# An LSTM's input products in groups of 32 steps with 26 outer products, instead of 24 steps with 20

## The chip, the cores and the metric

The kernel runs on one core of one Trainium2 chip. The metric is the device time of one execution in microseconds. In the texts and in the profile PE is TensorE (PEld its weight loads), DVE is VectorE, ACT is ScalarE, POOL is GpSimd and SP is SyncE, which issues all transfers here.

## What is computed

A residual around an LSTM layer in fp32: 32 sequences, 512 steps, 512 inputs, 512 hidden units, so 2048 gate columns. Cut to what matters:

```python
xW = einsum('ntd,dg->ntg', x, Wx) + b          # (32, 512, 2048)
def step((h, c), xw_t):
    a = xw_t + h @ Wh                          # the recurrent product
    i, f, o = sigmoid(a[:, :H]), sigmoid(a[:, H:2*H]), sigmoid(a[:, 2*H:3*H])
    g = tanh(a[:, 3*H:])
    c = f * c + i * g
    h = o * tanh(c)
    return (h, c), h
out = x + scan(step, (cond_1024, 0), xW)       # all h, added to x
```

`h @ Wh` can only be done step by step. `x @ Wx` has no such chain, and the kernel computes it for whole groups of steps ahead of their use, by a scheme that needs fewer multiplications than the plain product.

## The kernel before

**One step.** `h_part(t)` (L269) multiplies the last h by `wh_sb` into a PSUM bank that already holds that step's `x @ Wx + b` (16 matmuls of 512 columns, which the trace shows as 32). `cell(t)` follows (L284 to L295): two sigmoids and a tanh on ACT, the products and sums on DVE (`prod` L288, L289, L293), and the transposes (L295) that make the next step's h. While the cell runs, TensorE works on the stream of products for later steps (`emit_matmuls`, L548). TensorE's order in a step is the h part of the step, then a portion of the stream.

**The stream.** Steps 20 to 499 go in groups (`GS` steps, `NG` groups). A group's x is cut into blocks, and an outer bilinear algorithm of `R` slots gives its products: each slot multiplies one combination U of x blocks (`U_OF`, `U_SUMS`) by one combination V of weight blocks (`V_OF`, `V_SUMS`), and the output blocks are combinations W of the slots' results (`W_OF`, `W_SUMS`). Inside a slot a second algorithm with 7 products is used (`ROW`), so a slot is 7 products and a group `7 * R`. The position in the stream, `pos`, counts quarter products, 28 a slot. Each step issues as many as the group needs on average, rounded to even numbers: 22 or 24 a step.

**What DVE and ACT do for it.** `pair_sum` (L509 to L515) makes the four sums inside the x blocks. `u_op` (L453) makes a U. `evacuate` takes results out of the banks into buffers: three copies on ACT (L594, L603, L610) and three additions on DVE (L600, L604, L607) a slot. `w_op` (L418) makes the W. Finished output blocks are stored to DRAM (`store_blocks`, L434); `load_xw` (L663) brings them back three steps ahead of their use, and `seed_step` (L674) copies them into the step's bank on ACT. The bias comes in by copies on ACT (`seed_banks`, L578) that put a combination of bias rows in the bank of certain slots (`BIAS_OF`).

**Orders.** The order of work on each engine is the order of the program (`manual_schedule`). A budget decides how many W are made in a step: `room["dve"]` starts at 3800, each operation takes `150 + 1.05 * columns` off, and W are issued while more than 1000 is left; what does not fit waits in `wqueue`. In a step the evacuations come first, then U, pair sums and W, then the portion of the stream, then the cell. SP issues every transfer in the order of the program, and a transfer also waits for the one eight places earlier.

**V.** The V combinations are made once, at the start (`v_add`, L711), and stored to DRAM (`v_store`, L715): 768 + 128 KB for a sum, 384 + 128 KB for a slot whose V is a plain weight block (`V_DIRECT`). `load_v` (L639, L644) loads row after row into a ring of three.

**The head.** Steps 0 to 19 have `x @ Wx` computed plainly (`plain_block`, L202), since no group is ready. `HEAD_PLAINS` says which plain step is computed in which step. `keep` adds the bias on DVE to its bank: in place (L804), or into a buffer that waits in SBUF (L807), or into one that goes out to the DRAM tensor `kept` (L811, L812). The stream starts in step 6 with the portions of `HEAD_STREAM`; from `STREAM0` on a step has the steady portion. While the head runs, `load_group` (L500) loads the first x blocks, with the stores of V ahead of it on SP's queue.

**The tail.** The stream ends at step 472 (`END`); from 474 (`SPLIT`) on each step is done in two halves, so that the cell of one half runs beside the matmuls of the other. The last 12 steps are plain again (`plain_part`, L211), computed in portions as filler in the split steps, with weights that `late_loads` (L223) bring back in the steps listed in `LATE`. Their bias is added on DVE when the last portion of a step is done.

Of the kernel before, what the change touches and what calls it, by code (L numbers as in the profile page):

```python
# [24 lines left out]
GS = 24  # L25
NG = 20
TAIL = T - HEAD - NG * GS
R = 20
TAU = (1, 0, 2)
# [4 lines left out]
AHEAD = 28  # L34
# [3 lines left out]
LATE = (454, 456, 458, 460, 462, 470, 471)  # L38
# [6 lines left out]
V_FIRST = (1,)  # L45
V_NEXT = (3,)
V_STEPS = ((4, 5, 7), (8, 10), (11, 12, 13, 14), (15, 16, 17))
V_ROOMS = (0, 1, 2, 3, 4, 5, 2, 1, 3, 0, 4, 5, 3, 2)

U_SUMS = {6: {3: 1, 5: -1}, 7: {1: 1, 6: 1}, 8: {2: 1, 3: -1}, 9: {2: 1, 7: -1}, 10: {0: 1, 1: -1}, 11: {0: 1, 4: -1}}  # L50
U_OF = [
# [4 lines left out]
]  # L56
V_SUMS = {8: {0: 1, 4: 1}, 9: {3: 1, 7: 1}, 10: {5: 1, 8: -1}, 11: {6: 1, 8: -1}, 12: {6: 1, 9: 1}, 13: {5: 1, 9: -1}}
V_OF = [
# [4 lines left out]
]  # L63
W_SUMS = {
    20: {6: -1, 13: 1}, 21: {1: 1, 7: -1}, 22: {12: -1, 9: 1}, 23: {1: 1, 4: -1}, 24: {16: 1, 20: 1},
    25: {3: 1, 23: 1}, 26: {14: 1, 22: 1}, 27: {15: 1, 24: 1}, 28: {9: 1, 21: 1},
}
W_OF = [
# [3 lines left out]
]  # L72
BIAS_OF = {1: "b3", 3: "b1-b3", 8: "b2+b3", 11: "b2-b0", 13: "b0", 17: "b1-b0"}
# [29 lines left out]
def kernel(  # L103
# [22 lines left out]
    NC = 11  # L126
# [5 lines left out]
    ubuf = const.tile([P, 6, 7, P], F32, name="ubuf")  # L132
    xs0 = const.tile([P, 6, 8, P], F32, name="xs0")
    xs1 = r1[:, 0:6].rearrange("p a b c -> p (a b c)").rearrange("p (k s m) -> p k s m", k=6, s=8)
    xs = [xs0, xs1]
    xnat = const.tile([P, 3, TC, NJ, B], F32, name="xnat")
    seeds_own = const.tile([P, 2, W], F32, name="seeds_own")
    seeds = [r1[:, 6 + i // 2, i % 2 * 2 : i % 2 * 2 + 2].rearrange("p s c -> p (s c)") for i in range(4)]
    seeds += [seeds_own[:, i] for i in range(2)]
# [4 lines left out]
    xwd = [dram.tile([6, P, NJ, W], F32, name=f"xwd_{i}") for i in range(2)]  # L144
# [3 lines left out]

    EXTRA = {NC + 1: 3, NC + 2: 5, NC + 3: 1}
    extra_from = {NC + 1: (7, 0), NC + 2: (10, 5), NC + 3: (13, 0)}  # L150
    lent = []
    retired = []

    def buf_of(i):
        if i in EXTRA:
            return xs0[:, EXTRA[i]].rearrange("p s m -> p (s m)").rearrange("p (s c) -> p s c", s=4)
        return spare if i == NC else cbuf[:, i]

    def lend():
        for i, (made, row) in extra_from.items():  # L160
            if i not in lent and u_made[0] >= made and pos[0] >= 28 * row:
                lent.append(i)
                free_c.append(i)

    def retire():
        for i in lent:
            if i in free_c:
                free_c.remove(i)
                retired.append(i)
# [18 lines left out]
    late_r = xs0.rearrange("p k s m -> p k (s m)").rearrange("p k (s c) -> p k s c", s=4)  # L188

    def raw(blk):  # L190

        return (late_r if late_weights[0] and blk < 6 else r1)[:, blk]

    def plain_block(t, c, bank):

        ko, ki = divmod(c, 2)
        for j in range(NJ):
            w = raw(ko * 4 + j)
            dst = bank[j * B : (j + 1) * B]
            pieces = [(dst[:, 0:HW], w[:, 2 * ki + 1]), (dst[:, HW:W], w[:, 2 * ki])]  # L200
            for n, (d, m) in enumerate(pieces):
                nc.tensor.matmul(  # L202
                    d, x_of(t)[:, c], m, start=c == 0 and n == 0, stop=True, skip_group_check=True
                )
# [15 lines left out]
    def late_load(c, a, b):  # L220
        rows = wx[c].rearrange("p (j s c) -> p j s c", j=NJ, s=2)
        dst = late_r if a < 6 else r1
        return lambda: nc.sync.dma_start(  # L223
            out=dst[:, a:b, c % 2 * 2 : c % 2 * 2 + 2], in_=rows[:, a % 4 : a % 4 + b - a]
        )

    late_loads = [late_load(0, 0, 4), late_load(1, 0, 4), late_load(2, 4, 6), late_load(3, 4, 6)]
    late_loads += [lambda: nc.sync.dma_start(out=seeds_own[:, 0], in_=x[NCHUNK - 2][:, TC // 2 * P : TC * P])]
    late_loads += [late_load(2, 6, 8), late_load(3, 6, 8)]
# [89 lines left out]
    free_c = [*range(6), 8, 9, 10]  # L319
    last_x = []  # L320
    free_u = [2, 3, 4, 5, 0, 1]
# [11 lines left out]
    class Group:  # L333

        def __init__(self, g):
# [12 lines left out]
            for terms in [*U_SUMS.values(), *U_OF]:  # L348
                for i in terms:
                    if i > 5:  # L350
                        self.u_uses[i] = self.u_uses.get(i, 0) + 1
            self.u_slot = {}
            self.stored = [0, 0, 0]
# [91 lines left out]
    def u_block(gr, i):  # L445
        if i < 6:
            return flat(xs[gr.g % 2][:, i, 1:8])
# [290 lines left out]
    def v_slot(s):  # L738

        terms = V_OF[s]  # L740
        for i in terms:
            v_sum(i)
# [339 lines left out]
```

## Time and profile before

| | |
|---|---|
| time, median of 3 runs | 3108.54 us (3107.48 to 3110.77) |
| the profiled execution | 3108.65 us, of which span 3106.9 us |
| busy: PE, DVE, ACT, POOL | 3090.9, 2231.1, 1453.0, 232.3 us |
| moved by DMA | 760.40 MB, mean 245 GB/s |
| granted TensorE clock | full, in every slice of the span |
| starts of steps 0, 6, 20, 474 | 29.9, 88.5, 226.5, 2930.2 us |

The time of a run is 1 to 2 us longer than the span that the profile shows. A row of the list of groups gives line, engine and operation, out<-in with sizes, the count, then busy time and mean ns of one, then the idle time of the engine just before and what ended it. A row of the timeline gives start and length in us, and in brackets the idle time before. A row of the chain gives start, length and what the time went to. Busy TensorE is modelled from the ends of matmuls, so the starts of weight loads (PEld) are the better clock for its pace.

### The profile page before, as it was taken

The numbers are of one execution on the slowest core, as the hardware profiler recorded it, in microseconds if no ns is written. First come the engines' busy times: TensorE is split into PE (matmuls) and PEld (weight loads), VectorE is DVE, ScalarE is ACT, GpSimd is POOL, SyncE is SP. The second block draws the span as 40 slices with busy tenths as digits, with TensorE's granted clock in tenths as the row PEclk, the third lists the DMA queues.
The fourth block names the chain that finished last, engine by engine and source line by source line (L and its number), as shares of the span: only waits on it lengthen the run. The fifth ranks groups of instructions, "written<-read, shape, count | busy, mean of one in ns | idle before, by whom it ended". The sixth has DMA issues, their size and how long they took to land.

```text
span 3106.9 us, 109307 instructions
## 1 busy us (share of the span) xinstructions
PE 3090.9 (99%) x44064; PEld 1662.3 (54%) x44064; DVE 2231.1 (72%) x6217; ACT 1453.0 (47%) x5486; POOL 232.3 (7%) x508
## 2 busy tenths in 40 slices
PE   9999999999999999999999999999999999999999
PEld 6555555555555555555555555555555555555565
DVE  7587776767676777767676767677776767677644
ACT  1344444444444444444444444444444444444444
POOL 0000000000000000000000000000000000000010
PEclk9999999999999999999999999999999999999999
DMA  8788878787877778777877778787877777778630
GB/s 315 253 289 284 276 234 260 236 263 239 261 252 251 255 244 269 243 256 234 267 240 261 251 250 254 242 265 246 265 236 257 242 256 251 255 253 275 197 91 21
DMA packets 315274, 760.40 MB, mean 245 GB/s; under 512 B 50064, under 2 KB 98192, under 8 KB 314256
## 3 DMA queue, kind: packets, MB, share of 16 engines
q1 hardware_dynamic: 314768, 753.40, 74.6%
q8 instruction: 348, 5.70, 0.8%
q14 instruction: 158, 1.29, 0.1%
HBM read 576.26 MB, written 179.31 MB: 243 GB/s over the span
## 4 chain that ended last, share of the span: by engine, by line
PE 97%; DVE 1%; DMA 1%; ACT 0%; issue 0%; SPq 0%; DVEq 0%; ACTq 0%
PE gbank L269 54%; PE xbank L548 33%; PE bbank L548 5%; PE xbank L269 2%; PE xbank L211 1%; PE xbank L202 1%; PE gbank L202 1%; DMA vdram<-vring 0%; PE xbank L839 0%; DMA vring<-vdram 0%; PE bbank L202 0%; DVE prod L288 0%; DVE s L289 0%; DVE hbuf L293 0%; DVE ubuf L453 0%
## 5 line engine op out<-in xcount | busy, mean ns | idle before, releaser
L269 PE MATMUL gbank<-wh_sb,ht 128*32 128x512 f32 (+1 forms) x16256 | 1781.8, 576 | 1.9 <-DVE ht L295 1.1
L269 PEld LDWEIGHTS gbank<-wh_sb,ht 128*32 128x32 f32 x16256 | 609.6, 110 | 828.0 <-issue 704.1
L548 PE MATMUL xbank<-vring,ubuf 128*32 128x256 f32 (+1 forms) x15464 | 956.6, 364 | 4.7 <-ACT cbuf L610 4.0
L284 ACT ACTIVATE s<-gbank 128x128 f32<-128x128 f32 x978 | 274.7, 281 | 1278.7 <-PE gbank L269 1278.2
L548 PEld LDWEIGHTS xbank<-vring,ubuf 128*32 128x32 f32 x15464 | 591.7, 110 | 363.3 <-issue 188.6
L288 DVE TENSOR_TENSOR prod<-s 128x128 f32<-128x128 f32 x1024 | 293.9, 287 | 619.0 <-ACT s L285 618.9
L418 DVE TENSOR_TENSOR cbuf<-cbuf 128x1024 f32<-128x1024 f32 x401 | 482.5, 1216 | 1.4
L303 POOL TENSOR_TENSOR oc<-xnat,ht 128x128 f32<-128x128 f32 x504 | 232.1, 461 | 2835.6 <-DVE ht L295 1471.7
L291 ACT ACTIVATE tanh_c<-s 128x64 f32<-128x64 f32 x1024 | 262.3, 256 | 245.9 <-DVE s L289 241.8
L295 DVE STREAM_TRANSPOSE ht<-hbuf 128x64 f32<-128x64 f32 x1022 | 250.8, 245 | 74.7 <-DVE hbuf L293 1.4
L674 ACT COPY gbank<-xw 128x512 f32<-128x512 f32 x464 | 279.3, 602 | 0.2
L289 DVE TENSOR_TENSOR s<-prod 128x64 f32<-128x64 f32 x1024 | 230.4, 225 | 35.2
L293 DVE TENSOR_TENSOR hbuf<-o,tanh_c 128x64 f32<-128x64 f32 x1024 | 213.1, 208 | 28.8 <-ACT tanh_c L291 28.4
L594 ACT COPY cbuf<-xbank 128x512 f32<-128x512 f32 x370 | 216.0, 584 | 33.2 <-PE xbank L548 18.3
L285 ACT ACTIVATE s<-gbank 128x64 f32<-128x64 f32 x978 | 226.6, 232 | 0.0
L604 DVE TENSOR_TENSOR cbuf<-xbank,cbuf 128x256 f32<-128x256 f32 x370 | 151.6, 410 | 77.9 <-ACT cbuf L603 76.1
L548 PE MATMUL bbank<-vring,ubuf 128*32 128x256 f32 (+1 forms) x2704 | 200.6, 355 | 0.0
L548 PE MATMUL xbank<-vring,xs 128*32 128x256 f32 (+1 forms) x2472 | 173.8, 373 | 2.6 <-ACT xbank L578 1.9
L548 PE MATMUL xbank<-vring,r 128*32 128x256 f32 (+1 forms) x2480 | 173.8, 372 | 0.0
L286 ACT ACTIVATE o<-gbank 128x128 f32<-128x128 f32 (+1 forms) x508 | 155.5, 306 | 0.0
L607 DVE TENSOR_TENSOR cbuf<-xbank,cbuf 128x256 f32<-128x256 f32 x370 | 150.4, 407 | 0.0
L600 DVE TENSOR_TENSOR cbuf<-bbank,cbuf 128x256 f32<-128x256 f32 x370 | 150.0, 405 | 0.1
(114 smaller groups left out, 1804.4 us busy)
## 6 DMA issues: line engine op xcount, KB each, us to landing
vring<-vdram SPq DMA_DIRECT2D x320, 896.0 KB, 5.5
xw<-xwd SPq DMA_DIRECT2D x1920, 64.0 KB, 4.5
xwd<-cbuf SPq DMA_DIRECT2D x218, 512.0 KB, 4.5
out_dram<-oc SPq DMA_DIRECT2D x255, 128.0 KB, 3.6
xnat<-in_x_dram SPq DMA_DIRECT2D x62, 512.0 KB, 5.3
vring<-vdram SPq DMA_DIRECT2D x24, 768.0 KB, 6.5
vring<-vdram SPq DMA_DIRECT2D x32, 512.0 KB, 5.0
xs<-in_x_grouped_dram SPq DMA_DIRECT2D x10, 1536.0 KB, 8.8
```

The lines of the kernel that those rows point to most:

```text
L269: nc.tensor.matmul(dst[j * B : (j + 1) * B], state["ht"][:, k], m, start=False, stop=True, skip_group_check=True)
L284: nc.scalar.activation(s[:, u, 0:2], g[:, n_, 0:2], AF.Sigmoid)
L285: nc.scalar.activation(s[:, u, 2], g[:, n_, 3], AF.Tanh)
L288: nc.vector.tensor_mul(prod[:, u], s[:, u, 0:2], s[:, u, 2:4])
L289: add(nxt[:, u, 3], prod[:, u, 0], prod[:, u, 1])
L291: nc.scalar.activation(tanh_c[:, HALVES[u]], nxt[:, u, 3], AF.Tanh)
L295: nc.vector.transpose(ht[:, 2 * u : 2 * u + 2].rearrange("p q b -> p (q b)"), hbuf[:, HALVES[u]])
L303: (nc.gpsimd if t < T - 8 else nc.vector).tensor_add(oc[:, tt % 2], x_of(t), ht)
L418: op(c_of(dst), c_of(src), c_of(bb))
L548: nc.tensor.matmul(dst[j * B : (j + 1) * B, cols], left_of(gr, s, r)[:, j * B : (j + 1) * B], vring[:, row % 3, RIGHT[r], cols], start=sta ...
L594: nc.scalar.copy(t[:, 0:4:3], xb.rearrange("p (n c) -> p n c", n=2))
L674: nc.scalar.copy(bank_of(t), src)
```

## The change

Groups have 32 steps and 26 slots instead of 24 and 20, so there are 15 instead of 20. All tables of the outer algorithm are new: every U is now one sum or one plain block, there are 18 sums U instead of 13, 18 sums V instead of 14, and 16 output blocks with 38 operations L418 a group instead of 12 with 24. `BIAS_OF` has 11 slots instead of 6. Lines L418, L453, L509 to L515 of before are L407, L460, L491 to L497 after.

The x blocks come one row (two blocks, 0.5 MB) at a time into four places, three in `xs0` and one in `r1`, each row at its own position of the stream (`row_loads`), with its pair sums at fixed positions as well (`row_sums`); rows 0 and 1 of these lists share one set of sums of 512 columns, the others have sums of 256. What this frees of `r1` becomes six buffers for results. There are 8 buffers for U instead of 6. The stream starts to be steady at step 20 instead of 16, with other portions in the head, and ends four steps earlier; the split steps start at 470 instead of 474.

In the head ACT copies the bias into the banks of the plain steps (from those of step 0's list on) before their matmuls add to it; `keep` then does nothing for the banks that are used in place, and copies the parked ones out on ACT. Four of the six kept steps wait in the last place of `xs0`, which the third row of the first group is loaded into afterwards.

The core of the diff:

```diff
-GS = 24
-NG = 20
+GS = 32
+NG = 15
-R = 20
-TAU = (1, 0, 2)
+R = 26
+MB = 4
+TAU = (0, 1, 2, 3)
+XROWS = (2, 3, 0, 1)
+PLACES = ((0, 1, 2, 3), (2, 1, 0, 3))
-AHEAD = 28
+AHEAD = 32
-LATE = (454, 456, 458, 460, 462, 470, 471)
+LATE = (453, 455, 457, 463, 465, 467, 469)
-HEAD_STREAM = (0, 0, 0, 0, 0, 0, 36, 36, 60, 60, 60, 60, 64, 60, 64, 60)
+HEAD_STREAM = (0, 0, 0, 0, 0, 0, 36, 36, 60, 60, 60, 60, 60, 60, 60, 60, 60, 48, 40, 28)
-V_DIRECT = (0, 2, 6, 9, 18, 19)
-V_STEPS = ((4, 5, 7), (8, 10), (11, 12, 13, 14), (15, 16, 17))
+V_DIRECT = (2, 3, 7, 8, 15, 17, 21, 24)
+V_STEPS = ((13, 14, 15, 16), (17, 18, 19, 20), (21, 22, 23), (24, 25))
...
-    NC = 11
+    NC = 9
-    ubuf = const.tile([P, 6, 7, P], F32, name="ubuf")
+    ubuf = const.tile([P, 8, 7, P], F32, name="ubuf")
...
-    def plain_block(t, c, bank):
+    def plain_block(t, c, bank, seeded=False):
...
-                    d, x_of(t)[:, c], m, start=c == 0 and n == 0, stop=True, skip_group_check=True
+                    d, x_of(t)[:, c], m, start=c == 0 and n == 0 and not seeded, stop=True, skip_group_check=True
...
-    def load_group(g, a=0, b=6):
+    def load_row(g, q):
+        a = 2 * XROWS[q]
         nc.sync.dma_start(
-            out=xs[g % 2][:, a:b, 0:4],
-            in_=xg[g].rearrange("p (k s m) -> p k s m", k=6, s=4)[:, a:b],
+            out=pairs_at(PLACES[g % 2][q])[:, :, 0:4],
+            in_=xg[g].rearrange("p (k s m) -> p k s m", k=2 * MB, s=4)[:, a : a + 2],
         )
...
+    row_loads = [(R * g + p, g, q) for g in range(1, NG) for p, q in ((-10, 0), (-9.5, 1), (-2.5, 2), (3.5, 3))]
+    row_sums = [(5.5, 0, (3,))] * 4
+    for g in range(1, NG):
+        row_sums += [(R * g - 7.5, g, (0, 1))] * 4 + [(R * g - 0.5, g, (2,))] * 4 + [(R * g + 5.5, g, (3,))] * 4
+    def row_jobs(n):
+        while row_loads and pos[0] >= 28 * row_loads[0][0]:
+            load_row(*row_loads.pop(0)[1:])
+        while n and row_sums and pos[0] >= 28 * row_sums[0][0]:
+            pair_sum(*row_sums.pop(0)[1:])
+            n -= 1
...
+    def keep(p, bias_in=False):
         if p not in SEEDED:
-            add(bank_of(p), bank_of(p), bias_full)
+            if not bias_in:
+                add(bank_of(p), bank_of(p), bias_full)
             return
...
+        if bias_in:
+            nc.scalar.copy(dst, park_bank(p))
+        else:
+            add(dst, park_bank(p), bias_full)
...
-        jobs[5] = [lambda i=i: pair_sum(0, i) for i in range(4)] + [lambda: u_ahead(28)]
+        jobs[4] = [lambda: split_seeds((4,))] + [lambda: pair_sum(0, (0, 1))] * 4
+        jobs[5] = [lambda: u_ahead(28)] + [lambda: pair_sum(0, (2,))] * 4
...
+        for p in HEAD_PLAINS[0]:
+            nc.scalar.copy(plain_bank(p), bias_full)
...
             if t == 3:
-                load_seeds(((4, 3), (5, 1)), nc.sync)
-                load_group(0)
+                load_seeds(((4, 1),))
+                load_row(0, 0)
+                load_row(0, 1)
             if t == 5:
-                load_raw_seeds()
+                load_row(0, 2)
+                load_seeds(((1, 0), (3, 2), (2, 3)))
...
-                            plain_block(m, cc, bank)
+                            plain_block(m, cc, plain_bank(m), True)
                         if i == 0:
                             cell(t)
                             if t + 1 in SEEDED:
                                 seed_step(t + 1)
-                        keep(m)
+                        evacuate()
+                        keep(m, True)
...
+                for p in HEAD_PLAINS[t + 1] if t + 1 < len(HEAD_PLAINS) else ():
+                    nc.scalar.copy(plain_bank(p), bias_full)
...
-            if s_done.get(g, 4) < 4 and pos[0] >= 28 * (R * (g - 1) + 9) and room["dve"] > 900:
-                pair_sum(g, s_done[g])
-                s_done[g] += 1
+            row_jobs(1)
```

More of the change, by code (lines that the diff above doesn't have):

```diff
@@ L462, with u_flat, u_used @@
+        return None
+    def u_flat(gr, i):
+        b = u_block(gr, i)
+        return flat(ubuf[:, gr.u[i]] if b is None else b[:, 1:8])
+    def u_used(gr, i):
+        if i >= 2 * MB:
+            gr.u_uses[i] -= 1
+            if gr.u_uses[i] == 0:
+                free_u.append(gr.u[i])
     u_made = [0]
     def make_sum(gr, i):
-        if i > 5 and i not in gr.u:
-            for k in U_SUMS[i]:
-                make_sum(gr, k)
-            gr.u[i] = u_op(gr, U_SUMS[i])
+        if i < 2 * MB or i in gr.u:
+            return
+        (a, _), (b, sb) = sorted(U_SUMS[i].items(), key=lambda v: -v[1])
+        make_sum(gr, a)
+        make_sum(gr, b)
+        dst = take(free_u)
+        (add if sb > 0 else sub)(flat(ubuf[:, dst]), u_flat(gr, a), u_flat(gr, b))
+        room["dve"] -= cost_dve(896)
+        u_used(gr, a)
+        u_used(gr, b)
+        gr.u[i] = dst
@@ L787, in move_seeds @@
[L787 to L791 removed]
+            sub(seed_rows[i][:, HW:W], seed_rows[i][:, HW:W], seed_rows[i][:, 0:HW])
+    def late_seeds():
+        q = seed_rows
+        split_seeds((1, 2, 3))
+        sub(q[5], q[4], q[1])
+        sub(q[0], q[1], q[4])
+        sub(q[1], q[1], q[2])
+        add(q[3], q[0], q[3])
+        sub(q[0], q[0], q[3])
@@ L994 @@
             u_ahead(after)
[L995 to L1003 removed]
+            row_jobs(1)
             while wqueue and room["dve"] > 1000:
```

267 lines of the change are left out of this document (92 added, 175 removed), and 24 rows, old and new, of tables (U_OF, U_SUMS, V_OF, V_SUMS).

## The prediction

> **What bounds the kernel now.** I read the page first: the span, the busy shares and the chain that ended last.
>
> ```profile
> span 3106.9 us, 109307 instructions
> PE 3090.9 (99%) x44064; PEld 1662.3 (54%) x44064; DVE 2231.1 (72%) x6217; ACT 1453.0 (47%) x5486; POOL 232.3 (7%) x508
> PE 97%; DVE 1%; DMA 1%; ACT 0%; issue 0%; SPq 0%; DVEq 0%; ACTq 0%
> ```
>
> TensorE is busy for 99% of the span and 97% of the chain. The profiled run took 3108.65 us, 1.75 us more than its span and 0.1 us from the median of 3108.54; all sums below start from 3108.65. Next came the busy time by stretch (columns: PE, PEld, DVE, ACT, POOL, the granted clock, the DMA share, GB/s), to see where TensorE does wait.
>
> ```profile
> 80.00:100.00 20.00, 18.13 (x276) 12.04 (x271) 11.70 (x27) 4.57 (x18) 0.91 (x2) 1.00 0.91 328
> 100.00:120.00 20.00, 18.55 (x276) 9.37 (x267) 7.07 (x23) 5.72 (x21) 0.45 (x1) 1.00 0.62 200
> 120.00:140.00 20.00, 16.81 (x284) 10.16 (x280) 13.17 (x31) 7.90 (x21) 0.91 (x2) 1.00 0.60 196
> 600.00:1100.00 500.00, 500.00 (x6948) 263.87 (x6944) 367.95 (x1025) 241.27 (x903) 38.55 (x84) 1.00 0.79 254
> 3050.00:3107.00 57.00, 50.62 (x968) 30.59 (x960) 26.50 (x108) 23.91 (x116) 2.01 (x5) 0.99 0.06 19
> ```
>
> In the steady part TensorE never stops and the clock is full. Holes stand at 80 to 140 us, where the head goes over to the stream of products, and in the last 57 us, where no stream is left to fill the wait for the cell. So a product saved in the steady part is saved time, as long as VectorE keeps up, and head and tail are priced apart.
>
> The third view is one steady step (start, length, engine, line). The first weight load of L269 starts a step.
>
> ```profile
> 1631.86 0.37 PEld L269 LDWEIGHTS gbank<-wh_sb,ht 128*32 128x32 f32 x8
> 1636.20 0.29 DVE L288 TENSOR_TENSOR prod<-s 128x128 f32<-128x128 f32 x1 [0.90 <-ACT s L285]
> 1636.59 0.37 PEld L548 LDWEIGHTS bbank<-vring,ubuf 128*32 128x32 f32 x8
> 1637.02 0.81 PEld L548 LDWEIGHTS xbank<-vring,ubuf 128*32 128x32 f32 x16
> 1774.75 0.37 PEld L269 LDWEIGHTS gbank<-wh_sb,ht 128*32 128x32 f32 x8
> DVE prod L288 <- ACT s L285: 618.9, 505, 3.5
> ```
>
> Steps 256 and 280 start at 1631.86 and 1774.75: 24 steps in 142.9 us, 5.95 each. One product of the stream is 8 loads, 1636.59 to 1637.02: 0.43 us. The 24 steps hold 140 products, 60.4 us; the 82.5 left are 3.44 for each step's own matmuls. The last row is from the list of waits: VectorE stood idle ahead of the cell's first multiplication for 618.9 us, 505 times, 1.22 us a step. That idle time is what new VectorE work can use.
>
> **The products.** Before, 20 groups of 20 slots of 7 products are 2800; after, 15 of 26 slots are 2730. The steps that they serve are 480 both times, and head and tail compute 20 and 12 plain steps both times. 70 products by 0.431 (the step rows round it to 0.43; long runs of loads give 0.4316): **-30.2 us**, all on the path.
>
> **VectorE in the steady part.** The groups by shape give the prices.
>
> ```profile
> L418 DVE TENSOR_TENSOR cbuf<-cbuf 128x1024 f32<-128x1024 f32 x401 | 482.5, 1216 | 1.4
> L453 DVE TENSOR_TENSOR ubuf<-r 128x896 f32<-128x896 f32 x90 | 97.1, 1079 | 0.0
> L509 DVE TENSOR_TENSOR xs<-xs 128x768 f32<-128x768 f32 x10 | 9.4, 940 | 0.0
> L600 DVE TENSOR_TENSOR cbuf<-bbank,cbuf 128x256 f32<-128x256 f32 x370 | 150.0, 405 | 0.1
> L804 DVE TENSOR_TENSOR gbank<-gbank,bias_full 128x512 f32<-128x512 f32 x4 | 2.8, 699 | 8.5 <-PE gbank L202 8.5
> ```
>
> The output combinations (L418) go from 24 in each of 20 groups to 38 in each of 15: 570 for 480, +109 us. The input sums (L453) go from 260 to 270: +11. The pair sums are 60 of 128x512 (0.69 by the row of L804, same shape) and 120 of 128x256 (0.41) for 80 of 0.94: +15. Evacuations are 390 slots of three for 400: -12. Together +123 us, or 0.27 us in each of some 450 steps; the idle time ahead of the cell falls from 1.22 to 0.95 us a step. What counts is the worst step: work queued ahead of the cell has 1636.20 - 1631.86 = 4.34 us. The planner's budget of 3800 lets three evacuations, one input sum and one combination through (1.22 + 1.08 + 1.22 = 3.52), or three and two combinations (3.65). Both fit, so I take 0 and keep the other end for a rival. Steps of 22 quarter products, the ones without slack on TensorE, become 20 in 32 instead of 8 in 24; the cell just fits them now, so this too is 0, at worst +1.
>
> **Moved transfers in the steady part.** Rows of x go in 60 loads of 0.5 MB for 20 of 1.5, the same bytes. Output blocks are now loaded one step after their last store instead of 3 to 14, on SP's queue, and the rows of V queue behind that wait. A store lands some 2.4 us into the next step, its load some 2.7 us into the one after, and the copy that reads it comes 4 us later still. Priced at 0.
>
> **The head.** The V sums go from 14 to 18 and the raw stores from 6 to 8, all on SP's queue, with the first rows of x behind them.
>
> ```profile
> 33.00:58.00 25.00, 25.00 (x400) 18.02 (x396) 18.13 (x44) 4.09 (x21) 1.37 (x3) 1.00 0.95 341
> 62.50:90.50 28.00, 28.00 (x428) 19.42 (x424) 19.64 (x47) 4.09 (x21) 1.37 (x3) 1.00 0.94 332
> 79.35 10.90 DMA vdram<-vring
> vdram<-vring SPq DMA_DIRECT2D x7, 768.0 KB, 6.4
> vdram<-cbuf SPq DMA_DIRECT2D x6, 384.0 KB, 6.9
> 93.33 3.97 SPq L812 DMA_DIRECT2D kept<-cbuf  x6
> 97.35 1.73 SPq L777 DMA_DIRECT2D cbuf<-in_L_cond_b_dram  x3
> r<-in_x_grouped_dram SPq DMA_DIRECT2D x1, 512.0 KB, 4.2
> ```
>
> The first two rows show the transfers as the limit there (0.95 and 0.94 of the time, 336 GB/s), with a gap of 4.5 us between. The chain's piece ends the last store at 90.25. A sum costs 896 KB (768 + 128), a raw store 512 KB (384 + 128). Four more sums and two more raw ones, less 0.5 MB of x and 0.25 MB of seeds that now come later, are 3.9 MB: +11.7 us at 336 GB/s. The 4.5 us gap probably closes in part, as there are more sums to store: the last store lands at 97.5 (no gap) to 102, and I take 97. Behind it stand the rows of V, the output and the six kept stores (issued up to 97.30 before, 7.0 after the last V store) and then the third row of x, 4.2 for its transfer: at 108, rounded to 107 since some of these overlap. The sums of this row (4 x 0.41) stand on VectorE ahead of the cell of step 6; so do all instructions of that cell, and with it step 7.
>
> The Trainium skill's page HBM Reference, section Specifications (TRN2), says that a core which streams alone measures about 425 GB/s. By that figure, as an estimate, the 22 MB of the V phase would be out in 52 us instead of 65, and rival (a) below would hold. The two rows here disagree: 341 and 332 GB/s with the engines 0.95 and 0.94 full.
>
> ```profile
> 95.32 0.29 DVE L288 TENSOR_TENSOR prod<-s 128x128 f32<-128x128 f32 x1
> 98.56 1.07 PE L548 MATMUL xbank<-vring,xs 128*32 128x256 f32 x16 [1.87 <-ACT xbank L578]
> 101.39 0.35 PEld L269 LDWEIGHTS gbank<-wh_sb,ht 128*32 128x32 f32 x8
> 112.33 0.70 DVE L804 TENSOR_TENSOR gbank<-gbank,bias_full 128x512 f32<-128x512 f32 x1 [4.73 <-PE gbank L202]
> 131.14 0.34 PEld L269 LDWEIGHTS gbank<-wh_sb,ht 128*32 128x32 f32 x8
> ```
>
> Now the cell of step 6 multiplies at 95.32 and step 7 starts 6.07 later. After, it multiplies at 107 + 1.6 = 108.6, and step 7 starts some 5.6 later, as part of the stream no longer stands behind that cell: 114.2 for 101.39, **+12.8** (from +2, if the transfers keep pace with the sums, to +18 with the gap kept).
>
> In steps 7 and 8 (101.39 to 131.14, 29.75 us) VectorE's bias addition waits 4.73 us for a plain step's matmuls, with evacuations queued behind it, and TensorE then waits for those. ACT puts the bias in beforehand now, so this stall goes; 96 quarter products (10.4), the matmuls of two steps (6.9) and two plain ones (6.9) need 24.2, and with the cell of step 8, which is late next, I take 25.1: **-4.6** (0 to -5.6). In steps 9 to 16 the same kind of plan with one more step of stream: **+0.8**. Steps 17 to 19 hold 48, 40 and 28 quarter products, and VectorE's queue, priced with the rows above, holds 9.9, 9.2 and 5.6 us of work up to their cells, in steps of 8.6, 7.8 and 6.5 (3.44 and 0.108 for each quarter): **+4.0** (2.7, the bare excess, to 6).
>
> **The tail.** It starts 4 steps earlier, with the same plain filler.
>
> ```profile
> 3089.44 1.05 PEld L269 LDWEIGHTS gbank<-wh_sb,ht 128*32 128x32 f32 x24 [0.30 <-issue]
> 3091.91 0.28 ACT L284 ACTIVATE s<-gbank 128x128 f32<-128x128 f32 x1 [1.23 <-PE gbank L269]
> 3093.89 1.05 PEld L269 LDWEIGHTS xbank<-wh_sb,ht 128*32 128x32 f32 x24 [0.81 <-ACT o L286]
> 2912.54 0.37 PEld L269 LDWEIGHTS gbank<-wh_sb,ht 128*32 128x32 f32 x8
> 2914.15 1.18 SPq L223 DMA_DIRECT2D r<-in_L_cond_Wx_dram  x1
> r<-in_L_cond_Wx_dram SPq DMA_DIRECT2D x2, 512.0 KB, 4.2
> 2924.48 3.91 DVE L418 TENSOR_TENSOR cbuf<-cbuf 128x1024 f32<-128x1024 f32 x3
> ```
>
> A split step with next to no filler takes 3093.89 - 3089.44 = 4.45, where its matmuls alone are 16 loads by 0.2158, 3.45 as everywhere: four more such steps, **+4.0**. The seed copy that was late in step 510 has room: -0.4. The last late load of weights is issued in step 469 (LATE), whose own filler reads it 4.7 us after the step's start; before, such a load went out 1.61 after the start (2914.15 - 2912.54) and took 4.2, or more with another beside it: some 6.0 in, **+1.3**. Three combinations (3.91) stand ahead of the cell of step 470, a split step of 4.5 in which the cell's first activation stands 2.47 after the start (3091.91) and its multiplication would at about 2.6: 3.9 - 2.6, **+1.3**.
>
> **Sum.** -30.2 + 12.8 - 4.6 + 0.8 + 4.0 + 4.0 - 0.4 + 1.3 + 1.3 = -11.0: 3097.6 us, 0.35% less.
>
> **The rivals.** (a) *The head is not held up*: V stores keep pace (gap closed, faster transfers) or the row of x is not what comes last. Then 12.8 falls to 2 or less and step 7 is near 102: 3083 to 3087. For it: the gap of 4.5 us shows that VectorE, not the transfers, was late once. Against: 0.94 busy.
> (b) *VectorE becomes the bound* (the slower side): if an input sum joins two combinations ahead of the cell, 1.22 + 1.08 + 2.43 = 4.73 exceeds 4.34 by 0.39, and every such step loses that. There are 570 - 447 = some 123 steps with a second combination: 48 us, 3145. From 44 such steps on it is slower than 3114.8. Against: the budget of 3800; for: ACT's copies, which evacuations wait on, are more numerous too.
> (c) *The head costs what the products save*: gap kept (+5), steps 17 to 19 at 6, no gain in steps 7 and 8: 3097.6 + 5 + 2 + 4.6 = 3109, no change. That the products are not fewer can't be: the loops fix their count.
>
> **How the numbers follow.** A measurement of this kernel can tell about 0.2%, so faster ends at 3102.3 and slower begins at 3114.8. Forecast, within 3090 to 3102: 0.52; (a) 0.19; (c) and what lies between: 0.17; (b) 0.12. Faster is the forecast and (a), 0.71; same 0.17; slower 0.12. The range runs from the near end of (a), 3083, to (c) at 3109; it leaves out (b) and the far end of (a).
>
> **What the profile after would show.** Right: 3 or so stretches of 500 us in the middle with PE at 500; 2730 products; the third row of x landing at 104 to 110 and four pair sums of 128x256 ahead of the first multiplication of step 6's cell; step 20 at 245 us; no bias addition by VectorE after the first steps; 618.9 us of waits ahead of the cell down to about 490. Wrong: step 7 before 108 (a); PE idle in the middle with weight loads of L269's counterpart waiting for the transpose (b); a wait of the seed copy for its loaded block in the step after a store.

## The result, and the profile after

The changed kernel takes 3103.98 us (median of 20 runs, 3101.78 to 3106.88), the kernel before 3109.39 on the same chip: a ratio of 0.9983, 95% interval 0.9976 to 0.9990. Forecast were 3097.6 us and 0.35% less; it is 0.17% less, inside the range from 3083 to 3109. The profiled run took 3102.64 us. The page of it (span, busy time by engine, chain by engine):

```profile
span 3100.8 us, 108436 instructions
PE 3066.7 (99%) x43600; PEld 1636.5 (53%) x43600; DVE 2350.4 (76%) x6381; ACT 1473.7 (48%) x5530; POOL 236.9 (8%) x508
PE 97%; DMA 1%; DVE 1%; ACT 1%; SPq 0%; issue 0%; DVEq 0%; ACTq 0%
```

TensorE is busy 24.2 us less, VectorE 119.3 us more, and the span is only 6.1 us shorter: 18 us of that came back as idle TensorE. The busy time by stretch shows where (PE, PEld, DVE, ACT, POOL, granted clock, DMA share, GB/s):

```profile
80.00:100.00 20.00, 16.75 (x248) 11.32 (x240) 6.39 (x14) 4.37 (x16) 1.16 (x1) 1.00 1.03 367
100.00:120.00 20.00, 9.42 (x76) 3.12 (x80) 4.54 (x14) 4.53 (x10) 0.45 (x1) 0.57 0.57 178
200.00:250.00 50.00, 46.23 (x661) 21.74 (x656) 42.64 (x85) 20.48 (x67) 1.83 (x4) 0.97 0.80 268
600.00:1100.00 500.00, 499.96 (x6920) 261.32 (x6916) 395.62 (x1067) 245.19 (x915) 39.05 (x85) 1.00 0.78 253
```

The steady stretch shown is full, as before. TensorE stands still for 13.8 us between 80 and 120, and at the end of the head, 200 to 250, it loses 3.8 us more. In the second row the granted clock is 0.57; before it was 1.00 there.

The chain of events around step 7, in the timeline of the changed kernel:

```profile
93.64 3.76 SPq L791 DMA_DIRECT2D kept<-xs  x4
101.37 0.38 SPq L481 DMA_DIRECT2D xs<-in_x_grouped_dram  x1
105.12 0.43 DVE L491 TENSOR_TENSOR xs<-xs 128x256 f32<-128x256 f32 x1 [15.72 <-DMA xs<-in_x_grouped_dram]
106.59 0.28 DVE L278 TENSOR_TENSOR prod<-s 128x128 f32<-128x128 f32 x1
109.59 1.93 PE L545 MATMUL xbank<-vring,ubuf 128*32 128x256 f32 x16 [12.84 <-ACT cbuf L591]
110.02 0.20 PEld L545 LDWEIGHTS xbank<-vring,ubuf 128*32 128x32 f32 x4 [0.23 <-issue]
110.44 0.20 PEld L545 LDWEIGHTS xbank<-vring,ubuf 128*32 128x32 f32 x4 [0.23 <-issue]
114.64 0.20 PEld L259 LDWEIGHTS gbank<-wh_sb,ht 128*32 128x32 f32 x4 [0.23 <-issue]
140.41 0.39 PEld L259 LDWEIGHTS gbank<-wh_sb,ht 128*32 128x32 f32 x7
```

The chain has this row ahead of the load:

```profile
95.39 5.92 DMA kept<-xs
```

The last kept stores leave the place where the third row of x goes, so the load waits for them until 101.37; its sums, at 105.12, end a wait of 15.72 us on VectorE with the cell of step 6 behind them; TensorE waited 12.84 us for an evacuation on ACT that stands behind that cell's activations. Step 7 starts at 114.64. After the wait groups of four weight loads, for matmuls of 256 columns, start 0.42 us apart (110.02, 110.44), where half of that is the pace elsewhere.

### The profile page after: what moved, and what is told of

It is laid out like the page before. It is cut to its first block, busy times and chain, and to the rows that moved or that the text cites. A ratio compares the mean times of both kernels' runs of the same rounds, so it can differ in the third digit from the quotient of the medians.

```text
span 3100.8 us, 108436 instructions
## 1 busy us (share of the span) xinstructions
PE 3066.7 (99%) x43600; PEld 1636.5 (53%) x43600; DVE 2350.4 (76%) x6381; ACT 1473.7 (48%) x5530; POOL 236.9 (8%) x508
## 4 chain that ended last, share of the span: by engine, by line
PE 97%; DMA 1%; DVE 1%; ACT 1%; SPq 0%; issue 0%; DVEq 0%; ACTq 0%
PE gbank L259 53%; PE xbank L545 32%; PE bbank L545 5%; PE xbank L259 3%; PE xbank L192 1%; PE xbank L201 1%; PE gbank L192 1%; DMA xw<-xwd 0%; PE bbank L192 0%; DVE prod L278 0%; DMA kept<-xs 0%; DMA vring<-vdram 0%; PE xbank L818 0%; DVE s L279 0%; DMA r<-in_L_cond_Wx_dram 0%
## 5 line engine op out<-in xcount | busy, mean ns | idle before, releaser
L545 PE MATMUL xbank<-vring,ubuf 128*32 128x256 f32 (+1 forms) x13632 | 855.9, 369 | 18.9 <-ACT cbuf L591 12.8
L545 PEld LDWEIGHTS xbank<-vring,ubuf 128*32 128x32 f32 x13632 | 524.1, 110 | 318.0 <-issue 136.3
L545 PE MATMUL xbank<-vring,xs 128*32 128x256 f32 (+1 forms) x3216 | 210.1, 359 | 1.0 <-ACT xbank L575 1.0
L545 PE MATMUL xbank<-vring,r 128*32 128x256 f32 (+1 forms) x3216 | 208.2, 357 | 0.0
L545 PE MATMUL bbank<-vring,ubuf 128*32 128x256 f32 (+1 forms) x2608 | 185.3, 343 | 0.0
L545 PEld LDWEIGHTS xbank<-vring,r 128*32 128x32 f32 x3216 | 122.4, 110 | 80.2 <-issue 46.6
L545 PEld LDWEIGHTS xbank<-vring,xs 128*32 128x32 f32 x3216 | 123.2, 110 | 63.5 <-issue 24.4
L407 DVE TENSOR_TENSOR cbuf<-cbuf 128x1024 f32<-128x1024 f32 x128 | 155.8, 1219 | 0.7
L545 PEld LDWEIGHTS bbank<-vring,ubuf 128*32 128x32 f32 x2608 | 101.0, 110 | 68.8 <-issue 39.7
L407 DVE TENSOR_TENSOR r<-r,cbuf 128x1024 f32<-128x1024 f32 x111 | 134.7, 1221 | 0.9
```

Of the source, the lines that this page charges most:

```text
L407: op(c_of(dst), c_of(src), c_of(bb))
L545: nc.tensor.matmul(dst[j * B : (j + 1) * B, cols], left_of(gr, s, r)[:, j * B : (j + 1) * B], vring[:, row % 3, RIGHT[r], cols], start=sta ...
```

## The experiments

All are edits of one of the two kernels; each ratio is to the kernel before, run beside it, with its 95% interval. Lines left out of an edit are marked by `...`.

**The sums of the third row out of the cell's way.**

```diff
-        jobs[5] = [lambda: u_ahead(28)] + [lambda: pair_sum(0, (2,))] * 4
-        jobs[7] = [late_seeds]
+        jobs[5] = [lambda: u_ahead(28)]
+        jobs[7] = [late_seeds] + [lambda: pair_sum(0, (2,))] * 4
```

> The changed kernel with the four sums of the first group's third row moved from the jobs of step 5 to those of step 7, so that they no longer stand on VectorE ahead of the cell of step 6. Theory (the cell of step 6 waits for that row, and TensorE for the cell): the wait of 15.7 us goes, step 7 starts near 99 to 101 instead of 114.65, nothing later needs the row before step 9, and the total falls by 12 to 16 us, to 3088 to 3092 (ratio to the kernel before 0.993 to 0.995). Rival (the first rows of V, behind the same transfers on SP's queue, come just as late): step 7 or 8 then waits for a row of V, the start of step 9 moves by 4 us at most, total about 3100 (0.997).

3095.61 us, 0.9960 (0.9946 to 0.9973), between the theory and its rival. Both had a part in it. Step 7 starts at 100.91, as the theory said, but then takes 18.25 us. Its timeline:

```profile
103.09 0.38 SPq L481 DMA_DIRECT2D xs<-in_x_grouped_dram  x1
105.51 0.38 SPq L635 DMA_DIRECT2D vring<-in_L_cond_Wx_dram  x1
111.00 1.94 PE L545 MATMUL xbank<-vring,ubuf 128*32 128x256 f32 x16 [4.96 <-DMA vring<-in_L_cond_Wx_dram]
```

SP still stands at the load of the row until 103.09, with the rows of V behind it, and TensorE waits 4.96 us for one of those.

**The load itself behind the rows of V.** The sums stay in step 7, and in addition:

```diff
-            if t == 5:
+            if t == 7:
                 load_row(0, 2)
                 load_seeds(((1, 0), (3, 2), (2, 3)))
...
-        jobs[8] = [lambda: free_c.extend(range(NC + 1, NC + 7))]
+        jobs[8] = [late_seeds, lambda: free_c.extend(range(NC + 1, NC + 7))]
```

> The changed kernel with the sums of the third row moved to the jobs of step 7, as in the first experiment, and also the load of that row and of three seed rows issued at step 7 instead of step 5, so that rows 3 and 4 of V stand ahead of them on SP's queue; the sums of the seeds go to step 8. Theory (in the first experiment SP stood at this load, which waits for the kept stores, with the rows of V behind it): step 7 falls from 18.25 to 11 or 12 us and the total by 5 to 7 us against the first experiment, to 3088 to 3091 (0.993 to 0.994). Rival (the transfers are full there whatever their order): step 7 stays at 16 or more, total 3094 to 3097.

3089.49 us, 0.9937 (0.9925 to 0.9950). Steps 7 and 8 in it:

```profile
100.31 0.13 PEld L259 LDWEIGHTS gbank<-wh_sb,ht 128*32 128x32 f32 x4
111.08 0.33 PEld L259 LDWEIGHTS xbank<-wh_sb,ht 128*32 128x32 f32 x5
125.75 0.16 PEld L259 LDWEIGHTS gbank<-wh_sb,ht 128*32 128x32 f32 x4
```

Step 7 takes 10.77 us, its matmuls alone (6.9 with a plain step, 3.9 of stream). So the place of this row's load and sums, and of the three seed rows that moved with them, is worth 14.5 us against the changed kernel (3103.98 less 3089.49), more than the whole measured gain of the change.

**TensorE kept busy while it waits.** The changed kernel with 56 unused matmuls in step 6, on a bank that nothing uses then:

```diff
+                            for _ in range(14):
+                                for j in range(NJ): nc.tensor.matmul(xbank[3][j * B : (j + 1) * B], wh_sb[:, 0, 0, 0:B], ...)
```

> The changed kernel with 56 matmuls of 512 columns, whose results nobody reads, put on TensorE in step 6, where it waits 13 us for the cell. Theory (the granted clock falls to 0.50 in that wait and stays there into step 7): with TensorE busy the clock stays at 1.0, the first part of step 7 takes 3.4 us instead of 4.8, and step 8 starts 2 to 3 us sooner, total 3101 to 3102. Rival (the pace there is set by something else than the idle time): no difference, 3103 to 3105.

3099.37 us, 0.9969 (0.9958 to 0.9981). The same stretch, first of this kernel, then of the changed one:

```profile
112.00:118.00 6.00, 6.00 (x88) 2.58 (x82) 1.42 (x6) 1.79 (x8) 0.00 (x0) 1.00 0.37 111
```

```profile
112.00:118.00 6.00, 5.49 (x40) 1.97 (x44) 1.42 (x2) 1.56 (x3) 0.00 (x0) 0.51 0.39 112
```

The clock stays at 1.00 instead of 0.51, and twice as many matmuls fit. From step 6 to step 9 it is 48.16 us instead of 52.74 (starts at 88.72 and 136.88, and at 87.67 and 140.41). Not all of these 4.6 us are the clock's. Here the sums of the row come 15.4 us after the start of step 6, and in the changed kernel 17.5:

```profile
104.14 0.43 DVE L491 TENSOR_TENSOR xs<-xs 128x256 f32<-128x256 f32 x1 [13.71 <-DMA xs<-in_x_grouped_dram]
```

So 2.0 us of the difference are the row landing sooner; in the other kernels with this wait it varies from 16.6 to 17.9, and whether the unused matmuls have a part in it was not tried. From the first multiplication of that cell to step 7 it takes 7.12 us instead of 8.05, and step 7 falls from 12.40 to 10.77, its matmuls alone: 0.9 and 1.6, together some 2.6 us that the wait costs beyond its own length.

**Who puts the bias in.** Three kernels. In the first VectorE adds the bias in the changed kernel again:

```diff
-                            plain_block(m, cc, plain_bank(m), True)
+                            plain_block(m, cc, plain_bank(m))
...
-                        keep(m, True)
+                        keep(m)
...
-                for p in HEAD_PLAINS[t + 1] if t + 1 < len(HEAD_PLAINS) else ():
-                    nc.scalar.copy(plain_bank(p), bias_full)
```

> The changed kernel with the bias of the plain steps added by VectorE again, after their matmuls, and no copies of the bias into the banks by ACT; all else as changed. Theory: VectorE's additions wait for the matmuls again with evacuations behind them, steps 7 and 8 grow by about 4 us, total 3107 to 3109. Rival (the wait for the third row in step 6 covers it, and steps 7 and 8 have room): within 1 us of the changed kernel, 3103 to 3105.

3102.33 us, 0.9979 (0.9970 to 0.9987): no difference from the changed kernel, as the rival said. In the second the kernel before gets that part of the change alone, with the order that goes with it:

```diff
...
-                            plain_block(m, cc, bank)
+                            plain_block(m, cc, bank, True)
...
-                        keep(m)
+                        evacuate()
+                        keep(m, True)
...
+                for p in HEAD_PLAINS[t + 1] if t + 1 < len(HEAD_PLAINS) else ():
+                    nc.scalar.copy(plain_bank(p), bias_full)
```

> The kernel before with only that part of the change: ACT puts the bias into the banks of the plain steps, and copies parked ones out. Theory: steps 7 and 8 fall from 29.75 to about 25 us, total 4 to 6 us less, 3103 to 3105 (0.998 to 0.9987). Rival (the copies stand on ACT ahead of the cell's activations and cost what they save): no difference, 3108 to 3110.

3101.70 us, 0.9977 (0.9969 to 0.9986), a larger gain than its theory had. (With it some unused matmuls at the start go to another bank.) In the third the kernel before gets only the call that the change puts ahead of `keep`:

```diff
+                        evacuate()
                         keep(m)
```

> The kernel before with one call added: after a plain step in the head the finished results of the stream are evacuated before VectorE adds the bias, as the change does it; VectorE still adds the bias. Theory (the order on VectorE's queue made the stall, not who adds the bias): steps 7 and 8 fall from 29.75 to 25 or 26 us and the total by 4 to 7 us, to 3102 to 3105, as where ACT put the bias in. Rival (the gain is from ACT's share of the work): steps 7 and 8 stay over 29, total 3108 to 3110.

3106.08 us, 0.9991 (0.9982 to 0.9999). Steps 7 and 9 start here in the last two (first ACT's bias, then evacuation first):

```profile
99.59 0.34 PEld L269 LDWEIGHTS gbank<-wh_sb,ht 128*32 128x32 f32 x8
124.61 0.35 PEld L269 LDWEIGHTS gbank<-wh_sb,ht 128*32 128x32 f32 x8
```

```profile
100.83 0.35 PEld L269 LDWEIGHTS gbank<-wh_sb,ht 128*32 128x32 f32 x8
128.54 0.35 PEld L269 LDWEIGHTS gbank<-wh_sb,ht 128*32 128x32 f32 x8
```

For 29.75 us before, steps 7 and 8 take 25.02 with ACT's bias and 27.71 with the order alone; the latter lies between its theory and its rival. In the kernel before, then, 2.0 us come from the order on VectorE's queue, and 2.7 more when ACT has the bias too. In the changed kernel ACT's part brings nothing: the two steps take 25.77 us with it and 24.50 without, where their matmuls are 24.13, and what is above that lies in step 7, which begins in the low clock (until 117.91 with it, until 115.32 without). One more difference is in the sums of seeds, which stand on VectorE in step 8 of the kernel before, with two copies of them on ACT behind. These rows are of the kernel before:

```profile
125.99 1.99 ACT L789 COPY r<-cbuf 128x1024 f32<-128x1024 f32 x2 [6.00 <-DVE cbuf L785]
128.31 1.93 PE L548 MATMUL xbank<-vring,ubuf 128*32 128x256 f32 x32 [3.19 <-ACT cbuf L610]
```

ACT's copies wait 6.00 us for the sums, the evacuation that TensorE waits for stands behind them, and this is TensorE's longest wait there. The changed kernel has the sums in step 7 and no such copies. That this is why it does without ACT's bias is argued from the rows; no run changed it alone. Where the second experiment moved the sums back to step 8, that step went from 13.36 to 14.67 us.

Put side by side, the change without ACT's bias is at 0.9979, ACT's bias without the new groups at 0.9977, and both together at 0.9983. One small part of the change, alone in the kernel before, is thus worth as much as all of it.

**VectorE's cover in the steady part.** One, two and three more sums of 256 columns a step ahead of the cell, each number in 128 steps.

```diff
+    extra = const.tile([P, HW], F32, name="extra")
...
             while wqueue and room["dve"] > 1000:
                 w_op()
+            if 60 <= t < 444:
+                for _ in range(1 + (t - 60) // 128):
+                    add(extra, bias_full[:, 0:HW], bias_full[:, HW:W])
```

> The changed kernel with more work on VectorE ahead of the cell, results unused: one sum of 256 columns (about 0.41 us) in each of steps 60 to 187, two in steps 188 to 315, three in steps 316 to 443. By the prediction the queue ahead of the cell is at most 3.65 us of 4.34: one more sum costs nothing (128 steps at 5.89 us), two cost up to 0.13 us in the fullest steps, 0 to 10 us in 128 steps, three cost up to 0.5 us, 20 to 60 us. By the rival in which VectorE already binds, one sum alone costs 0.2 to 0.4 us a step, 25 to 50 us in 128 steps.

3174.32 us, a single run. Steps 60, 188, 316 and 444 in it:

```profile
490.58 0.27 PEld L260 LDWEIGHTS gbank<-wh_sb,ht 128*32 128x32 f32 x8
1246.97 0.27 PEld L260 LDWEIGHTS gbank<-wh_sb,ht 128*32 128x32 f32 x8
2017.50 0.19 PEld L260 LDWEIGHTS gbank<-wh_sb,ht 128*32 128x32 f32 x8 [0.38 <-ACT cbuf L608]
2823.26 0.19 PEld L260 LDWEIGHTS gbank<-wh_sb,ht 128*32 128x32 f32 x8 [0.87 <-ACT r L608]
```

The three parts take 756.4, 770.5 and 805.8 us; in the changed kernel they take 754.3, 754.4 and 754.1. One sum costs 2 us in 128 steps, two 16, three 52. The cover is more than one such sum and less than two, as the prediction had it (0.69 us), and two cost somewhat more than expected (0 to 10). Its rival (b), by which one sum alone would have cost 25 us or more, is out.

**The end of the head: stores behind the rows of V.** In steps 16 to 19 the stores of finished blocks are kept back until the rows of V of that portion are issued; `issue` sends what `store_blocks` has put aside.

```diff
...
                         emit_matmuls(m)
+                        if hold[0]:
+                            load_v_ahead()
+                            issue()
```

> The changed kernel with the stores of finished output blocks in steps 16 to 19 issued behind the rows of V instead of ahead of them on SP's queue; the work of all other engines is the same. Theory (in step 17 SP stands some 10 us at a store that waits for VectorE's combination, and the row of V behind it comes late): step 17 falls from 13.9 to about 10, total 3 to 5 us less, 3099 to 3101 (0.997). Rival (VectorE is overloaded there and the late cell is what counts, as the prediction had it): step 17 stays over 13 and the total within 1 us of the changed kernel.

3101.30 us, 0.9980 (0.9972 to 0.9989), the same as the changed kernel. What it undoes is this, in the changed kernel:

```profile
224.56 2.35 DVE L407 TENSOR_TENSOR cbuf<-cbuf,r 128x1024 f32<-128x1024 f32 x2
225.80 0.37 SPq L423 DMA_DIRECT2D xwd<-cbuf  x1
227.81 0.41 SPq L640 DMA_DIRECT2D vring<-vdram  x1
231.21 0.64 PE L545 MATMUL xbank<-vring,ubuf 128*32 128x256 f32 x8 [1.33 <-ACT gbank L670]
233.70 2.59 PE L545 MATMUL xbank<-vring,ubuf 128*32 128x256 f32 x24 [1.86 <-DMA vring<-vdram]
```

SP stands at a store until the first of these two combinations is done and the store goes out at 225.80, and a row of V behind it lands 1.86 us late. With the stores kept back step 17 falls from 13.87 to 9.95 us, but step 18 rises from 7.78 to 11.42: the cell there waits for the combinations. Steps 17 to 19 together stay at 28.7 us: the stall moved by one step, so the store was only its messenger.

**The combinations of steps 16 to 19 made short** (128 of 1024 columns, the rest left out; `hold[0]` is set in steps 16 to 19).

```diff
...
-        op(c_of(dst), c_of(src), c_of(bb))
+        n = 128 if hold[0] else 4 * HW
+        op(c_of(dst)[:, 0:n], c_of(src)[:, 0:n], c_of(bb)[:, 0:n])
```

> The changed kernel with the combinations of steps 16 to 19 done on 128 of their 1024 columns, so that the rest of those output blocks is left out; every instruction, transfer and wait stays. Theory (VectorE's combinations set the length of steps 17 to 19, through the late cell and the late stores): 13 combinations less by about 1 us each, steps 17 to 19 fall from 28.7 to 23 or 24 us. Rival (the rows of V come late by themselves): they stay over 27.

Steps 17 and 20 in it:

```profile
222.22 0.13 PEld L259 LDWEIGHTS gbank<-wh_sb,ht 128*32 128x32 f32 x4
248.04 0.16 PEld L259 LDWEIGHTS gbank<-wh_sb,ht 128*32 128x32 f32 x4
247.39 1.07 PE L548 MATMUL xbank<-vring,xs 128*32 128x256 f32 x16 [2.63 <-DMA vring<-vdram]
```

3101.12 us, a single run. Steps 17 to 19 take 25.8 us instead of 28.7, between the theory and its rival; their matmuls are 22.8. Step 17 falls to 8.79 (8.6 alone), so VectorE's combinations make its stall. The 2.6 us that are left stand in step 19 at a row of V; why that row is late there was not tried.

**ACT's seed copies earlier.**

```diff
-                        seed_banks(m)
+                        seed_banks(max(m, 24))
```

> The changed kernel; in the head ACT's copies of bias rows into the banks of slots are given out 24 quarter products ahead of the stream instead of 12 where a portion is 12. Theory (11 seeded slots in 26 instead of 6 in 20 make TensorE wait for such a copy in steps 10, 11, 16 and 17, about 4 us in all, which the prediction priced at nothing): steps 10, 11 and 16 fall from 11.51, 11.10 and 10.70 to near 9.9, the total by 2 to 4 us, 3100 to 3102. Rival (the copy is late because it waits for the bank's evacuation): those steps stay as they are, 3103 to 3105.

3100.27 us, 0.9970 (0.9960 to 0.9981). Step 11 falls from 11.10 to 9.91, steps 10 and 16 stay at 11.51 and 10.70, so the theory holds for one of three. Two waits of the changed kernel, the first in step 6, the second in step 10:

```profile
112.51 2.79 PE L545 MATMUL xbank<-vring,xs 128*32 128x256 f32 x24 [0.98 <-ACT xbank L575]
158.13 1.93 PE L545 MATMUL xbank<-vring,ubuf 128*32 128x256 f32 x32 [1.32 <-ACT xbank L575]
```

The second stays: ACT goes without a pause from the end of the cell through the evacuations to that copy, with the edit as without, which fits the rival. The first is gone, and from the first multiplication of step 6's cell to step 7 it takes 6.84 us instead of 8.05, so 1.2 us more are the edit's. The rest of what steps 6 and 7 lose, 1.5 us, is a row that lands 0.7 sooner after the start of step 6 and a low clock that ends at 114.55 instead of 117.91.

**Three edits together, twice.** The load and sums of the third row as in the second experiment, the earlier seed copies, and `LATE = (453, 455, 457, 463, 465, 466, 467)`; then a sister with the seed rows left at step 5.

> The changed kernel with three edits together: the third row's sums at step 7 with its load and the seed rows issued at step 7 (as in the experiment that gave 3089.5), the seed copies of the head 24 quarter products ahead, and the last late loads of weights in steps 466 and 467 instead of 467 and 469. Expected: 3089.5 less 2 to 4 for the seed copies and less 0.7 for step 469 (from 6.5 to 5.8): 3085 to 3087. If the gains do not add up, 3089.

> As the kernel with three edits together, but the three seed rows are loaded at step 5 and their sums made in step 7, as in the changed kernel; only the load of the third row is moved to step 7. Expected, if the sums of the seeds are what makes step 8 take 14.7 instead of 13.4: 1 to 1.3 us less than its sister, 3084 to 3086. If the seed rows hold up the rows of V: step 7 at 12 or more, 1 us more than its sister.

3085.02 us, 0.9927 (0.9915 to 0.9940), and 3086.73 us, 0.9933 (0.9920 to 0.9945); the intervals overlap, so the sister is told apart by its steps alone. The gains add up. Steps 6 and 11 fall by 1.2 us each against the second experiment, step 469 to 5.87 and step 470 to 5.97. In the sister step 8 takes 13.36 instead of 14.68, but step 7 12.65 instead of 10.77, with 1.5 us of waits for rows of V: the seed rows hold these up. Three stretches of the first one:

```profile
80.00:100.00 20.00, 20.00 (x304) 13.15 (x299) 9.59 (x24) 9.00 (x26) 1.62 (x2) 1.00 1.04 367
100.00:120.00 20.00, 20.00 (x320) 13.68 (x316) 10.81 (x34) 6.08 (x22) 0.95 (x2) 1.00 0.75 263
200.00:250.00 50.00, 46.01 (x628) 20.88 (x624) 43.64 (x99) 21.05 (x71) 2.75 (x6) 0.97 0.75 230
```

The hole between 80 and 120 is gone and the clock is full; that at the end of the head is still there. It is 0.6% faster than the changed kernel and 0.7% faster than the one before.

## Why the prediction was right, and where it was not

The time lies in the range, but above 3102.3, where the prediction let "faster" end: 3090 to 3102 had a chance of 0.52, and what came had 0.17. In the profile the gain is 6.1 us for a forecast of 11.0. Of the three conditions of rival (c), one came, the cost of steps 17 to 19.

*Products, -30.2.* Right. Between steps 28 and 460 the changed kernel gains 26.5 us; 63 of the 70 products lie there, 27.2.

*VectorE in the steady part, 0.* Right: TensorE is at 500 of 500, VectorE is busy 119 us more against 123 forecast, and its waits ahead of the cell fell as said:

```profile
DVE prod L278 <- ACT s L275: 478.4, 459, 7.2
```

*The transfers there, 0.* Right to within 1 us in this profile, but the sign of being wrong that the prediction named is there. ACT's seed copies wait for their loaded blocks, 6.1 us in five waits where the kernel before has none, and the longest makes step 33 0.9 us longer than its matmuls:

```profile
332.88 0.59 ACT L670 COPY gbank<-xw 128x512 f32<-128x512 f32 x1 [3.35 <-DMA xw<-xwd]
```

In eight of the ten other kernels with the new groups step 28 is 0.8 to 2.3 us longer, by such a wait.

*The late third row, +12.8.* Right that the row holds up the cell, and the size came out by errors that cancel: the sums at 105.12 against "107", step 7 at 114.64 against 114.2; step 6 is 14.1 us longer. The volume was right (3.9 MB more from 20 to 100 us), the rate was not: the last V store landed at 92.75 instead of 97, since the gap closed and the transfers ran faster than 336 GB/s:

```profile
33.00:92.75 59.75, 59.75 (x924) 42.60 (x920) 44.92 (x94) 18.62 (x65) 5.93 (x6) 1.00 1.01 362
```

Rival (a)'s first condition thus came in part, without its time. For the load waits some 4 us at the head of SP's queue, from the end of the last kept store's issue (97.40) until the stores that leave its place have landed; the sum did not have that wait, and the second experiment shows that the load's position in the queue is what matters. From the cell's multiplication to step 7 it took 8.05 us instead of 5.6, with a seed copy and the low clock in it. The Trainium skill's HBM Reference, section Specifications (TRN2), with 425 GB/s for a core that streams alone, is not borne out in this phase: it moved 362 GB/s with the DMA engines full, though the 8 us from 20 to 28, ahead of it, had 419.

*Steps 7 and 8, -4.6.* The number is right (-4.0), the reason is not. It held that ACT's taking over of the bias ends the stall. In the kernel before that is so for 2.7 us, with 2.0 from the order on VectorE's queue; in the changed kernel the stall ends without ACT's part, and the 1.6 us above the matmuls are the low clock. Behind the wait of 4.73 us on VectorE that it read, TensorE waits only 0.69 us; its long wait there, 3.19, stands behind the copies of seeds on ACT, which the prediction did not name.

*Steps 9 to 16, +0.8.* Too small, and for a reason that was not priced. They take 83.0 us, 3.8 more than their matmuls, where it was 1.5 before: +2.3. The prediction took over the plan of before and did not price that 11 of 26 slots instead of 6 of 20 need their bank seeded: TensorE waits for such a copy in steps 10, 11 and 16 (1.6, 1.2 and 0.8 us longer).

*Steps 17 to 19, +4.0.* Right in mechanism, too small: 28.7 us, 5.8 more than the matmuls, where before there was no excess. Short combinations take 2.9 of these away, close to VectorE's bare excess (2.7). It did not have the rows of V that come late, of which one still costs 2.6 us then.

*The tail, +6.2.* Right: from step 469 to the end it takes 202.4 us, and before from step 473 182.6, a difference of 19.8; four steps' matmuls are 13.8, so 6.0 is left. Its parts came out otherwise: the late load costs 0.7 and not 1.3 (step 469 takes 6.52, and 5.87 with the load sooner), and step 470 is 2.1 longer than a split step and not 1.3. Both waits that were named are there, the load landing 0.88 us late in step 469, and three combinations ahead of step 470's cell:

```profile
2904.61 0.41 PE L201 MATMUL xbank<-r,seeds_own 128*32 128x256 f32 x2 [0.88 <-DMA r<-in_L_cond_Wx_dram]
2906.32 2.47 DVE L407 TENSOR_TENSOR r<-r,cbuf 128x1024 f32<-128x1024 f32 x2
2908.72 1.22 DVE L407 TENSOR_TENSOR cbuf<-cbuf 128x1024 f32<-128x1024 f32 x1
```

*The clock.* Not in the prediction. It forecast a wait of TensorE of about 13 us and no cost beyond it; some 2.6 us more were measured, 0.9 at the end of step 6 and 1.6 in step 7.

So the 4.9 us that are missing from the forecast gain lie in step 6 (1.3), steps 7 and 8 (0.6), 9 to 16 (1.5), 17 to 19 (1.8) and the steady part (0.7), less 1.0 in the other places. Step 20 starts at 252.1 instead of the 245 that was expected. A larger share of the products' 30 us could have been kept by the place of one row's load and sums, as the last experiments show.

## What to carry to other kernels

Price the head and tail of a longer group as closely as its steady part: here 30 us of saved products met some 24 us of lost time, nearly all at the ends, 14 of them in one step, where a load and four small sums stood ahead of a cell which did not need them. In queues that run in order, look at each operation with a late input and ask what stands behind it that has no need of it. A stall that goes when one edit is made may have had two causes: do each part alone, in both kernels. And measure the small parts of a large change alone before crediting the large one: here the bias on ACT alone, in the kernel before, gave as much as everything together.

## What was not expected of the hardware

TensorE's granted clock fell to 0.50 during a wait of 13 us, and it stayed there from 100.85 to 117.91, some 8 us after the first matmul at 109.59; groups of four loads for 256 columns were 0.42 us apart instead of 0.2158. It fell again at 233.97, after two waits of 1.33 and 1.86 us. The low stretches that end inside a kernel are 3.41, 6.83, 13.65 or 17.07 us long in all the profiles, multiples of 3.41, and in the changed kernel the two begin 39 times 3.41 us apart, as if on a fixed grid. Four windows of that grid (columns as above):

```profile
111.09:114.50 3.41, 2.42 (x26) 0.99 (x24) 1.42 (x2) 1.38 (x3) 0.00 (x0) 0.50 0.48 132
114.50:117.91 3.41, 3.41 (x24) 0.98 (x20) 0.00 (x0) 0.59 (x1) 0.00 (x0) 0.50 0.22 74
230.55:233.96 3.41, 0.90 (x15) 0.36 (x19) 2.55 (x9) 1.71 (x5) 0.46 (x1) 1.00 0.90 331
233.97:237.38 3.41, 3.41 (x40) 1.74 (x36) 3.38 (x4) 0.96 (x2) 0.00 (x0) 0.50 1.04 339
```

The first window has 1.0 us without a matmul, and the clock stays low after it; the second has none, and the clock comes back. The third has 2.5 us without one, and the next is at half clock. The same cut through all fourteen profiles, from 8 us on, leaves no exception: at full clock a window with up to 1.99 us idle kept it, and one with 2.14 or more halved it for the next; at half clock up to 0.54 us idle brought it back, and 0.96 or more did not. The busy times are modelled, and no run was made to try these bounds. The longest wait of TensorE for another engine in the kernel before, 3.19 us, falls into two windows with 1.2 and 2.0 us of it, and the clock stayed at 1.00.

The Trainium skill's page TensorE: Matmul & The Clock Gate, section What's actually happening, says that the clock is halved after an idle window of about 3.4 us and restored after a busy one, and that the windows run on without regard to the kernel. The trace agrees, with its 3.41 us, and shows that a window need be neither wholly idle nor wholly busy.
